# Reshaping and moving the piecewise loads of layer 1: pieces of 128 partitions by 1 KB, issued at one step of a block

## The chip, the cores and the metric

The kernel runs on one core of one Trainium2 chip. A core has five engines that work side by side, each through its own queue of instructions in order: TensorE (PE in the profile, with its weight loads as PEld), VectorE (DVE), ScalarE (ACT), GpSimd (POOL) and SyncE (SP), which here issues nearly all the transfers (DMA). The metric is the device time of one execution in microseconds; lower is better.

## What is computed

The input x has 8 images of 512 channels by 32 x 32 points (t = 1024 tokens), all float32. Two layers follow each other, each with a group normalization first and a residual sum at the end. Cut to what matters:

```python
# layer 0: xf = _gn(x)
qkv = einsum('oc,bct->bot', qkv_w, group_norm(xf)) + qkv_b      # 8 heads of 64 channels
a = softmax(q.T k / sqrt(64)) v
x = x + einsum('oc,bct->bot', proj_w, xf + a) + proj_b
# layer 1: xf = _gn(x)
attn = einsum('bhdq,bhdT->bhqT', q, k) * scale                  # q, k, v = w_q xf, w_k xf, w_v xf
attn = softmax(einsum('gh,bhqT->bgqT', w_head, attn))           # the heads are mixed before the softmax
attn = instance_norm(attn) * gamma + beta                       # over queries and keys of one head
out = einsum('bhqT,bhdT->bhqd', attn, v).reshape(b, t, c)
x = x + (out @ w_proj.T + b_proj)
```

The mixing of the heads is what makes layer 1 heavy in transfers: scores of all 8 heads have to stand on the partitions of one matmul, and they are brought there by DMA.

## The kernel before

Layer 0 (lines up to 1261) runs first over all images and leaves its result in DRAM, in the tensors x1_0 to x1_7. Layer 1 (from 1264) then takes the images b = 0 to 7 one after the other. The order of instructions on each engine is the order in which the program writes them (a manual schedule, line 576); a framework adds the waits that the tiles need.

**One image of layer 1.** The 1024 queries are cut into 8 blocks p of 128. The loop runs over p = 0 to 8, and in each over four steps t = 0 to 3 (`step`, line 1839). Block p makes the scores of its queries, and mixes, exponentiates, flips and sums up what block p - 1 made, so the work is spread over three blocks:

- `scores` (1624) makes one of eight parts of block p; two parts in each step. ScalarE copies them from PSUM to a tile raw, one for each half kh of the keys (line 1643; two raw tiles in all, so that a block's copies wait until the transfers out of the block before are done).
- `regroup` (1645, issue on line 1648) brings a slice s of raw into the tile re by two transfers of 256 KB, r = 0 and 1, 128 rows of 2 KB each. Step 1 regroups (kh, s) = (0,0) and (0,1), step 2 (0,2), step 3 (0,3) and then (1,0), (1,1), (1,2), (1,3): 16 transfers in a block, ten of them in step 3. There is one tile re, so slice s is overwritten only after the mix of the block before has read it.
- `mix` (1658) mixes the heads: slice t of block p - 1 in step t. Its matmuls (1665) read re, ScalarE takes the exponential (1675).
- `flip` (1680) and `moments` (1692) are VectorE's transposes (1687) and statistics (1698); `values` (1702) multiplies with v (1714); `leave` (1722) copies the result out. `totals` (1746) of block p - 2 comes in step 1 with a reciprocal on line 1761, and the transfer of its inverse sums, rzb, is issued by GpSimd (1771).

Block 8 has no scores of its own; it only ends block 7, and next to it run the first products of the next image's k projection (`k_go`; matmuls on line 1383).

**The pieces.** While image b runs, the inputs of image b + 1 are loaded in pieces of 128 KB. The list `self.pieces` holds them in order: 16 pieces of y (`y_piece`, 1334: x1 of the next image, 2 MB, into the tile y), then 14 pieces of the k weights (`left_piece`, 1299: 1.8 MB of combined weights, from DRAM into the tile left_k). Image 7 has no successor and loads 8 pieces of w_proj instead (`p_piece`, 1324). `piece(n)` (1652) issues the next n. It is called at the end of steps 1 and 2 of every block from 1 on:

```python
                if p >= 1 and t in (1, 2):
                    self.piece(2 if p < 5 or t == 2 else 3)
```

So blocks 1 to 4 issue the 16 y pieces, four in each, and blocks 5 to 7 the 14 k pieces, five, five and four. In image 7 blocks 1 and 2 issue the eight w_proj pieces, and no block after them issues any. y is normalized in block 5 (`normalize1`, at slots 20 to 23), and left_k is read from the last step of block 7 on.

A y piece covers 32 partitions with 4 KB each (a whole row of 1024 tokens); a k piece and a w_proj piece cover 64 partitions with 2 KB each.

**The queue.** Pieces and regroups are issued by SP in program order. In the compiled program each transfer of SP also waits until the eighth before it has landed, so at most eight are under way. A regroup that waits for scores holds up everything behind it on SP.

Of the kernel before, what the change touches and what calls it, by code (L numbers as in the profile page):

```python
# [18 lines left out]
P = 128  # L19
# [448 lines left out]
def tile_two_attention_layers(  # L468
# [20 lines left out]
    B, C, T = x_d.shape  # L489
    H = w_head.shape[0]  # L490
    D = C // H
# [11 lines left out]
    x1_d = [dram.tile([C, T], F32, tag=f"x1_{b}", name=f"x1_{b}") for b in range(B)]  # L503
# [190 lines left out]
    with ExitStack() as l0:  # L694
# [21 lines left out]
        for c in range(NCC):  # L716
# [5 lines left out]
        HC = C // 2  # L722
# [4 lines left out]
        left_d = {  # L727
            which: dram.tile([P, 7 * 2 * HC], F32, tag=f"left_{which}", name=f"left_{which}")
            for which in SOURCES
        }  # L730
        left_t = {}

        def left_tile(which, b):
            t = wpool.tile([P, 7, 2, HC], F32, tag="left", name=f"left_{which}_{b}")
            left_t[which] = t
            return t
# [527 lines left out]
    with ExitStack() as l1:  # L1264
# [21 lines left out]
        y_t, qo_t, k_t, v_t = ({0: t["1"]} for t in (n_t, q_t, k_t, v_t))  # L1286
        w_t = {}
# [3 lines left out]
        HC = C // 2  # L1291
# [7 lines left out]
        def left_piece(key, i):  # L1299

            if i == 0:
                left_tile(key)
            f, r = i // 2, i % 2 * D
            return nc.sync.dma_start(
                out=w_t[key][r : r + D, f],
                in_=left_d[key[0] + "1"][r : r + D, f * 2 * HC : (f + 1) * 2 * HC],
            )

        def load_left(key, t=None):
# [14 lines left out]
        def p_piece(i):  # L1324

            if i == 0:
                left_tile(("p", B - 1))
                w_t["p", B - 1] = w_t["p", B - 1][:, :NCC]
            c, r = i // 2, i % 2 * D
            return nc.sync.dma_start(  # L1330
                out=w_t["p", B - 1][r : r + D, c], in_=w_projT[c * P + r : c * P + r + D]
            )

        def y_piece(b, i):

            if i == 0:
                y_t[b] = shared.tile([P, NCC, T], F32, tag="n", name=f"y_{b}")
            c, r = i // 4, i % 4 * 32
            return nc.sync.dma_start(
                out=y_t[b][r : r + 32, c], in_=x1_d[b][c * P + r : c * P + r + 32, :]  # L1340
            )

        def normalize1(b, c):
# [101 lines left out]
        def k_leave():  # L1445
            for fn in due:
                fn()
            due.clear()
# [167 lines left out]
        class Attention1:  # L1616
# [222 lines left out]
            def step(self, p, t, ag):  # L1839

                if p >= 1 and t == 3:
                    self.mix(p - 1, 3)
                if p < NT:
                    self.scores(p, 2 * t)
                    self.scores(p, 2 * t + 1)
                if t == 1 and p >= 2:
                    self.totals(p - 2)
                if t == 1 and p >= 1:
                    self.flip(p - 1, 0)
                    self.moments(p - 1, 0)  # L1850
                if t == 0 and p >= 2:
                    self.values(p - 2, 0, 1)
                    self.leave(p - 2, 0)
                if p >= 1 and t < 3:
                    self.mix(p - 1, t)
                ag.run(4 * p + t - 0.5)
                if 1 <= t <= 2 and p >= 2:
                    self.values(p - 2, 1, t - 1)
                    if t == 2:
                        self.leave(p - 2, 1)  # L1860
                if t == 3 and p >= 1:
                    self.values(p - 1, 0, 0)
                if t == 0 and p >= 2:
                    self.sums(p - 2)
                    if p % 2 == 0 and p >= 4:
                        self.divide(p // 2 - 2)
                k_leave()
                if p >= 1 and t:
                    self.flip(p - 1, t)
                    self.moments(p - 1, t)  # L1870
                if p < NT:
                    for kh, s in (
                        (), ((0, 0), (0, 1)), ((0, 2),), ((0, 3), (1, 0), (1, 1), (1, 2), (1, 3)),
                    )[t]:
                        self.regroup(kh, s)
                if p >= 1 and t in (1, 2):
                    self.piece(2 if p < 5 or t == 2 else 3)
                ag.run(4 * p + t)

        def load_wv(b):  # L1880
# [7 lines left out]
        for b in range(B):  # L1888
# [10 lines left out]
            if more:  # L1899
                a.pieces += [lambda i=i: y_piece(b + 1, i) for i in range(4 * NCC)]  # L1900
                a.pieces += [lambda i=i: left_piece(("k", b + 1), i) for i in range(14)]
                for c in range(NCC):
                    ag.at(20 + c, lambda c=c: normalize1(b + 1, c))

                def k_go(*ms):
                    if not kp:
                        kp.append(k_projection(b + 1))
                    for m in ms:
                        kp[0].products(m)
                        due.append(lambda m=m: kp[0].leave(m))  # L1910

                kp = []
                ag.at(4 * NT - 0.5, lambda: right_tile(b + 1))
                ag.at(4 * NT - 0.5, lambda: k_go(1))
                ag.at(4 * NT, lambda: right_y(b + 1, [0, 1]))
                ag.at(4 * NT + 0.5, lambda: k_go(2))
                ag.at(4 * NT + 1, lambda: right_y(b + 1, [2, 3]))
                ag.at(4 * NT + 1, lambda: left_p(b))
                ag.at(4 * NT + 1.5, lambda: k_go(6))
                ag.at(4 * NT + 2.5, lambda: k_go(7))  # L1920
            else:
                a.pieces += [lambda i=i: p_piece(i) for i in range(2 * NCC)]
# [113 lines left out]
```

## Time and profile before

| what | value |
|---|---|
| median of 3 runs | 4119.6 us (4113.11 to 4122.85) |
| the profiled execution | 4120.51 us |
| its span, first to last instruction | 4118.7 us |
| mean granted TensorE clock | 0.992 |
| transfers `re<-raw` | 1024 of 256 KB |
| transfers `y<-x` in pieces | 112 of 128 KB |
| transfers `left_k<-left_k` in pieces | 98 of 128 KB |
| share of queue 1 (SP's) of 16 DMA engines' span | 43.7% |

How to read the profile: the page gives busy time per engine, and the span in 40 equal slices, each digit being tenths of busy time (9 is 90% or more). "Waits" list who waited for whom: engine, line of the waiter, what released it, total us, how often, the longest. "Windows" list the busy us of each engine in a stretch of time, with the clock granted to TensorE, the mean busy share of the 16 DMA engines, and GB/s moved. A timeline row gives start, length, engine, line, operation, tiles, and in brackets the idle time ahead and what ended it. Lines are those of the kernel. Busy times of matmuls are modelled, so a busy TensorE isn't TensorE at its peak.

### The profile page before, as it was taken

The page shows a single profiled execution, that of the slowest core. Times are in us where ns is not written, and L with a number is a line of the kernel's source. Part 1 is how long each engine was busy: PE and PEld are TensorE (multiplying, and loading weights), DVE is VectorE, ACT ScalarE, POOL GpSimd, SP SyncE. Part 2 cuts the span into 40 slices and gives each one's busy share as a digit, 9 for nine tenths or more (in the row PEclk, how much of TensorE's full clock was granted, in tenths as well). Part 3 has the DMA queues.
Part 4 walks back from the last instruction along what each step waited for, and adds up shares of the span by engine and source line. Part 5 has one row for each costly group of instructions (what it writes and reads, how often), then busy time and mean ns, then how long its engine had stood idle before and what let it go on. Part 6 is the DMA issues. An engine that isn't in the chain of part 4 may idle for free. (4 is left out here: it accounts for less than half of the span.)

```text
span 4118.7 us, 96170 instructions
## 1 busy us (share of the span) xinstructions
PE 3945.7 (96%) x41932; PEld 1822.9 (44%) x41932; DVE 2876.9 (70%) x4340; ACT 1961.1 (48%) x2431; POOL 71.2 (2%) x126
## 2 busy tenths in 40 slices
PE   8999999999999999999999999998998999999997
PEld 4353535353534343334434434444444444445344
DVE  4748484757575666648859768769678589498596
ACT  1717272636354544427437347256166165174273
POOL 0000000000000000000000000000000000000000
PEclk9999999999999999999999999999999999999998
DMA  3313131212121111139649558469288287397384
GB/s 128 106 51 109 49 114 44 88 47 88 47 85 49 56 62 65 70 106 216 175 115 220 147 146 209 137 162 218 97 190 212 88 209 183 113 215 191 108 207 119
DMA packets 251101, 519.12 MB, mean 126 GB/s; under 512 B 49840, under 2 KB 57008, under 8 KB 244016
## 3 DMA queue, kind: packets, MB, share of 16 engines
q1 hardware_dynamic: 244128, 497.96, 43.7%
q0 software_dynamic: 6544, 14.94, 1.7%
q8 instruction: 331, 5.42, 0.6%
q14 instruction: 98, 0.80, 0.1%
HBM read 197.16 MB, written 46.92 MB: 59 GB/s over the span
## 5 line engine op out<-in xcount | busy, mean ns | idle before, releaser
L1698 DVE BATCH_NORM_STATS2 bn<-e 128x6 f32<-128x512 f32 x1024 | 631.5, 671 | 0.0
L1643 ACT COPY raw<-s 128x1024 f32<-128x1024 f32 x480 | 465.7, 1022 | 322.0 <-PE s L1631 158.4
L1687 DVE STREAM_TRANSPOSE et<-e 128x2048 f32<-128x2048 f32 x256 | 585.6, 2288 | 34.5 <-ACT e L1675 34.5
L1086 ACT ACTIVATE e<-s 128x1024 f32<-128x1024 f32 x512 | 497.2, 1026 | 233.2 <-PE s L1081 232.8
L1675 ACT ACTIVATE e<-m 128x1024 f32<-128x1024 f32 x512 | 496.6, 1022 | 196.0 <-issue 58.8
L1714 PEld LDWEIGHTS a<-et,v 128*64 128x64 f32 x16384 | 499.7, 138 | 194.1 <-issue 193.3
L1631 PE MATMUL s<-k,q 64*64 64x512 f32 x4096 | 534.4, 616 | 43.2 <-ACT e L1675 37.5
L1714 PE MATMUL a<-et,v 128*64 128x64 f32 x16384 | 531.7, 224 | 4.9 <-DVE et L1687 4.9
L1094 DVE TENSOR_TENSOR zacc<-zacc,e 128x1024 f32<-128x1024 f32 x384 | 468.8, 1221 | 90.2 <-ACT e L1086 68.0
L1081 PE MATMUL s<-q,k 64*64 64x512 f32 x4096 | 490.1, 593 | 2.3 <-ACT e L1086 2.3
L1107 PE MATMUL a<-e,v 64*64 64x512 f32 x4096 | 484.1, 589 | 0.0
L1665 PE MATMUL m<-re,wmix 32*32 32x512 f32 x8192 | 368.6, 612 | 83.1 <-DMA re<-raw 34.0
L1631 PEld LDWEIGHTS s<-k,q 64*64 64x64 f32 x4096 | 124.1, 133 | 364.7 <-ACT e L1675 162.5
L1107 PEld LDWEIGHTS a<-e,v 64*64 64x64 f32 x4096 | 156.7, 133 | 282.8 <-issue 282.5
L1081 PEld LDWEIGHTS s<-q,k 64*64 64x64 f32 x4096 | 147.9, 133 | 275.2 <-issue 240.5
L1458 PE MATMUL pv<-wv,y 128*128 128x512 f32 x480 | 212.1, 597 | 0.0
L1665 PEld LDWEIGHTS m<-re,wmix 32*32 32x32 f32 x8192 | 80.8, 103 | 212.2 <-ACT raw L1643 92.1
L1730 ACT COPY q<-a 64x256 f32<-64x256 f32 x256 | 94.0, 367 | 146.9 <-PE a L1714 144.1
L1458 PEld LDWEIGHTS pv<-wv,y 128*128 128x128 f32 x480 | 89.3, 190 | 117.7 <-issue 109.5
L1761 DVE RECIPROCAL rz<-z 32x32 f32<-32x32 f32 x64 | 22.1, 346 | 160.7 <-PE z L1750 150.9
L1462 ACT COPY v<-pv 128x512 f32<-128x512 f32 x30 | 17.6, 586 | 218.5 <-PE pv L1458 218.5
L1092 DVE TENSOR_TENSOR zacc<-e,e 128x1024 f32<-128x1024 f32 x64 | 78.3, 1224 | 55.9 <-ACT e L1086 55.9
(314 smaller groups left out, 3948.7 us busy)
## 6 DMA issues: line engine op xcount, KB each, us to landing
re<-raw SPq DMA_DIRECT2D x1024, 256.0 KB
left_q<-left_q SPq DMA_DIRECT2D x17, 1792.0 KB
left_p<-left_p SPq DMA_DIRECT2D x17, 1792.0 KB
left_k<-left_k SPq DMA_DIRECT2D x10, 1792.0 KB
x<-in_x_dram SPq DMA_DIRECT2D x32, 512.0 KB
rzb<-zd SPq DMA_DIRECT2D x128, 128.0 KB
x<-x SPq DMA_DIRECT2D x64, 256.0 KB
left_v<-left_v SPq DMA_DIRECT2D x8, 1792.0 KB
```

The lines of the kernel that those rows point to most:

```text
L1081: nc.tensor.matmul(ps[c * D : c * D + D, m], k[r, hp, k0 : k0 + D], q[r, hp, ts(f, FB)], start=True, stop=True,)
L1086: nc.scalar.activation(e[i], ps, AF.Exp, scale=S0 * S0)
L1094: nc.vector.tensor_add(zacc[g], zacc[g], e[i])
L1107: nc.tensor.matmul(acc[g][a][m * D : m * D + D], v[rows, kc, ts(2 * hp + m, D)], e[i][rows, m], start=(kc == 0), stop=(kc == NG - 1),)
L1458: nc.tensor.matmul(ps[:, m], y_t[b][:, c, ts(2 * i + m, P)], w[:, c], start=(c == 0), stop=(c == NCC - 1),)
L1631: nc.tensor.matmul(ps[c * D : c * D + D, m], qo_t[b][r, p, hp, ts(c, D)], k_t[b][r, hp, ts(kh, FB)], start=True, stop=True,)
L1643: nc.scalar.copy(dst, ps)
L1665: nc.tensor.matmul(ps[a // 2][c * 32 : c * 32 + 32, a % 2].rearrange("p (r kb k) -> p r kb k", r=2, k=32), wmix[rows].rearrange("p g i -> ...
L1675: nc.scalar.activation(e[:, :, 2 * h : 2 * h + 2].rearrange("p r a k -> p a r k"), ps[h].rearrange("p a (r k) -> p a r k", r=2), AF.Exp,)
L1687: nc.vector.transpose(self.et[p, u].rearrange("p kb (r st a) g q -> p st kb r (a g q)", r=2, st=2)[:, st], self.e[p, s].rearrange("p r a ( ...
L1698: nc.vector.bn_stats(self.bn[p][:, s, a], e[:, :, a].rearrange("p r k -> p k r"))
L1714: nc.tensor.matmul(acc[two * D : two * D + D, s].rearrange("p (x q) -> p x q", q=4), v_t[b][:, kb, ts(g, D)], et[:, kb, :, g], start=(kb = ...
```

## The change

Two things change, both for the pieces of layer 1 alone.

Their shape: every piece now covers all 128 partitions with 1 KB each. A y piece is a quarter of the tokens of 128 channels, a k piece or a w_proj piece half of the columns of 128 rows. The number of pieces, their order, their bytes and the tiles they fill stay the same.

Their place: they are issued at the end of step 0, four in blocks 1 to 4, five (in the end four) in blocks 5 to 7, rather than at the ends of steps 1 and 2. Step 0 regroups nothing. On SP they therefore stand behind the last regroups of the block before, (1,0) to (1,3), and ahead of the first of the block's own, (0,0). The order of instructions on the other engines stays.

```diff
@@ left_piece
-            f, r = i // 2, i % 2 * D
+            f, h = i // 2, i % 2
             return nc.sync.dma_start(
-                out=w_t[key][r : r + D, f],
-                in_=left_d[key[0] + "1"][r : r + D, f * 2 * HC : (f + 1) * 2 * HC],
+                out=w_t[key][:, f, ts(h, HC)],
+                in_=left_d[key[0] + "1"][:, (2 * f + h) * HC : (2 * f + h + 1) * HC],
             )
@@ p_piece
-            c, r = i // 2, i % 2 * D
+            c, h = i // 2, i % 2
             return nc.sync.dma_start(
-                out=w_t["p", B - 1][r : r + D, c], in_=w_projT[c * P + r : c * P + r + D]
+                out=w_t["p", B - 1][:, c, ts(h, HC)], in_=w_projT[ts(c, P), ts(h, HC)]
             )
@@ y_piece
-            c, r = i // 4, i % 4 * 32
+            c, r = i // 4, i % 4
             return nc.sync.dma_start(
-                out=y_t[b][r : r + 32, c], in_=x1_d[b][c * P + r : c * P + r + 32, :]
+                out=y_t[b][:, c, ts(r, HC)], in_=x1_d[b][ts(c, P), ts(r, HC)]
             )
@@ step
-                if p >= 1 and t in (1, 2):
-                    self.piece(2 if p < 5 or t == 2 else 3)
+                if p >= 1 and t == 0:
+                    self.piece(4 if p < 5 else 5)
                 ag.run(4 * p + t)
```

Here P = 128, D = 64, HC = 256, and `ts(i, n)` is the slice from i n to (i + 1) n.

## The prediction

> **What bounds the kernel now.** I read the page first: engines, slices, costliest groups.
>
> ```profile
> PE 3945.7 (96%) x41932; PEld 1822.9 (44%) x41932; DVE 2876.9 (70%) x4340; ACT 1961.1 (48%) x2431; POOL 71.2 (2%) x126
> ...
> DMA  3313131212121111139649558469288287397384
> GB/s 128 106 51 109 49 114 44 88 47 88 47 85 49 56 62 65 70 106 216 175 115 220 147 146 209 137 162 218 97 190 212 88 209 183 113 215 191 108 207 119
> ```
>
> TensorE is busy 96% of the span, so only its gaps can be won. The DMA row rises to 8 and 9 tenths in the second half: that is layer 1, from about 1800 us on, the only part that the change touches. So I asked who waits for transfers there (the waits of ScalarE and TensorE from 1800 us on; columns: total us, times, longest).
>
> ```profile
> ACT raw L1643 <- DMA re<-raw: 116.0, 37, 4.3
> ...
> PE m L1665 <- DMA re<-raw: 34.0, 23, 3.8
> ```
>
> These are regroups (`re<-raw`), not pieces: the pieces can cost time only by delaying regroups. The control for that is in the trace itself. Image 7, the last, loads nothing for a successor; its pieces (w_proj) end in block 2, so its blocks 3 to 6 run without pieces. I cut the span at the reciprocal of L1761, which falls in step 1 of each block, and asked for busy time by window (columns: window, length, busy us of each engine with counts, granted clock, DMA share, GB/s). First two of image 7 without pieces, then two of image 3 with y pieces, then the sum line for the 14 such windows (blocks 3 and 4 of images 0 to 6), then the sum line for the seven windows of block 6 with k weight pieces.
>
> ```profile
> 3961.12:3983.41 22.29, 21.60 (x454) 11.11 (x454) 20.37 (x32) 16.68 (x21) 1.15 (x2) 1.00 0.81 202
> 3983.41:4005.76 22.35, 21.58 (x454) 11.05 (x453) 21.50 (x33) 16.73 (x21) 1.15 (x2) 1.00 0.83 203
> ...
> 2765.64:2789.77 24.13, 21.61 (x454) 11.11 (x455) 21.51 (x32) 16.61 (x21) 1.15 (x2) 1.00 0.92 215
> 2789.77:2813.35 23.58, 21.79 (x454) 11.29 (x454) 21.20 (x32) 16.67 (x21) 1.15 (x2) 1.00 0.90 215
> ...
> sum 329.81, PE 303.74 PEld 156.14 DVE 298.94 ACT 232.90 POOL 16.16; mean PE 21.70 PEld 11.15 DVE 21.35 ACT 16.64 POOL 1.15
> ...
> sum 162.71, PE 149.96 PEld 77.57 DVE 142.61 ACT 115.13 POOL 8.08; mean PE 21.42 PEld 11.08 DVE 20.37 ACT 16.45 POOL 1.15
> ```
>
> The engines do the same work in all of them; only length and DMA share differ. Image 7's four windows average 22.36 us; the 14 with four y pieces 329.81/14 = 23.56; the seven with five k pieces 162.71/7 = 23.24. So pieces cost 1.20 us in a y block and 0.88 in a k block. Length times DMA share, averaged over the rows: 18.33 us of DMA work without pieces, 21.41 with y pieces, 21.36 with k pieces. A y piece thus costs 3.08/4 = 0.77 us of all 16 engines, a k piece 3.03/5 = 0.61. About 4 us of a block are free of DMA work without pieces; with them the block is nearly bound by transfers.
>
> Block 7 into 8 is worse, because block 8 has no scores to cover a late regroup. TensorE's timeline of image 3, then of image 6, at that place (start, length, what, idle before):
>
> ```profile
> 2881.33 2.02 PE L1665 MATMUL m<-re,wmix 32*32 32x512 f32 x32 [4.05 <-issue]
> 2883.28 5.44 PE L1383 MATMUL pk<-y,left_k 128*128 128x512 f32 x8
> ...
> 3761.83 1.30 PE L1665 MATMUL m<-re,wmix 32*32 32x512 f32 x32 [2.35 <-DMA re<-raw]
> 3763.05 3.70 PE L1383 MATMUL pk<-y,left_k 128*128 128x512 f32 x8
> ```
>
> After a 4 us gap the same eight matmuls take 5.44 us instead of 3.70: the wait is paid again in clock. The seven intervals at this place average 26.09 us, the best is 24.06.
>
> **What the Trainium skill says.** "SBUF — State Buffer", section "Door 1: The DMA port swizzle": partitions 0 to 31 and 0 to 63 reach the same 8 of 16 ports, 0 to 127 reach all (189, 196 and 328 GB/s at 1 MiB). The trace agrees in the mean: 131 KB in 0.77 us is 170 GB/s for 32-partition pieces and 215 for 64. For the new shape there is a witness: the layer 0 weight blocks are 128 rows of 1 KB, 128 KB each. The window in which eight of them run almost alone:
>
> ```profile
> 73.60:77.00 3.40, 3.40 (x10) 1.49 (x9) 1.59 (x3) 1.17 (x2) 0.00 (x0) 1.00 0.93 303
> ```
>
> 303/0.93 = 326 GB/s of busy time, 0.40 us a piece. "DMA: Bandwidth & Descriptors", section "Issuing engines are not separate DMA queues": all transfers end on the same 16 engines and interleave; the summed shares above fit. Same page, "Why small descriptors are slow (HBM only)": about 3 cycles more per packet; my estimate from it is 4 x (1024/32 + 3) = 140 against 131 cycles, 7% for cutting 4 KB into 1 KB. No run here shows it alone. "TensorE: Matmul & The Clock Gate", section "Why this matters for your kernels": no idle gaps over about 3 us; the 5.44 against 3.70 us agrees.
>
> **The change part by part.** Nothing is added or removed: as many pieces of 128 KB, as many bytes; the orders of TensorE, VectorE, ScalarE and GpSimd are the same, only SP's differs.
>
> Shape. Priced alone, a piece falls to 0.40 us (row above). Beside regroups it stretches: image 7's blocks move about 200 GB/s at a share of 0.82, 244 GB/s of busy time, so 131/244 = 0.54 us. I take 0.5 and keep both ends. A y block then has 4 x 0.5 = 2.0 us of piece work for 3.08, a k block 2.5 for 3.03. What that is worth: read as a threshold, about 2 us of piece work are hidden now (3.08 - 1.20 = 1.88; 3.03 - 0.88 = 2.15) and the rest costs one for one, so a y block wins up to 1.20 and a k block about 0.4. Read in proportion (1.20/3.08 and 0.88/3.03), they win 0.42 and 0.15.
>
> Place. Now two pieces stand between the regroups of step 1 and that of step 2 and two (or three and two) before those of step 3, ahead of the regroups that the next block's first mix and first raw copy wait for. After the change all stand on SP between the eight regroups that end step 3 and the first regroup of step 1. The eight are ahead of them in the queue, so the urgent ones lose a competitor. Each transfer on SP waits for the eighth before it, so the four pieces issue as those eight land, when DMA would run dry until step 1's raw copies are done. What is moved past: the four regroups of step 1 and the two of step 2 (first used a block later) now stand behind the pieces, by at most 4 x 0.54 = 2.2 us, nothing if DMA is free. GpSimd's rzb load of step 1 meets the same backlog; its value is used blocks later. On SP 16 regroups of about 0.6 us and four or five issues of 0.4 to 0.6 fill some 12 us of 22: SP itself isn't the bound. No new wait comes to bear: the y tile's last reader (v_pair in block 0) is issued a block earlier, the k tile's an image earlier. y is complete two steps sooner for its normalization, the k weights two steps sooner for their product. Taking place and shape together I put a y block at 0.9 won and a k block at 0.4. For block 7 into 8, where a gap also costs clock, I take 1.2 of the 26.09 - 24.06 = 2.03 us; both ends 0.4 and 2.03.
>
> Sum. Per image 0 to 6: blocks 1 to 4 (y) 4 x 0.9 = 3.6; blocks 5 and 6 (k) 0.8; block 7 1.2: 5.6 us, times 7 = 39. Image 7: two blocks of four w_proj pieces, 64 partitions each; block 2 measured 23.01, 0.65 over 22.36; I take 0.5 each, 1. Together 40 us. The profiled execution is 4120.5 us (span 4118.7), within 1 us of the median 4119.6: 4120.5 - 40 = 4080. In proportion only: 4 x 0.42 + 2 x 0.15 + 0.4 = 2.4, times 7 = 17 us, 4103. Everything won: 4 x 1.20 + 2 x 0.88 + 2.03 = 8.6, times 7, plus 1.3 = 61 us, 4059.
>
> **Rivals.**
> 1. The pieces vanish: in their new place they fall wholly into the DMA gap. For it: image 7's 4 us of free DMA time a block against 2.0 to 2.5 of pieces. Against: the gap isn't all at that place. 4059, with 4052 to 4064 around it.
> 2. Nothing changes: the ten regroups of step 3 set the waits by themselves, and the pieces only fill time beside them. For it: the waits name regroups alone. Against: image 7's blocks, same regroups, are 1.20 us shorter. 4120, within 8.
> 3. Slower: a transfer beside the regroups pays per row, not per byte. Place: the 16 engines in blocks 1 to 7. Regroup rows of 2 KB take about 17.2 us (18.33 less some 1.1 for rzb) over 128 rows per engine, 0.134 us each; if a 1 KB row costs as much, a piece of 8 rows per engine costs 1.07 us. With hidden room used up, that is 4 x 0.30 = 1.2 us more in a y block, 5 x 0.46 = 2.3 in a k block, 1.8 in block 7: 11.2 an image, 79 in all, 4199. It decides from 0.70 us a piece on (the mean of 16 at 0.77 and 14 at 0.61), 0.087 us a row. For it: no 1 KB row in this trace runs beside regroups. Against: alone, such rows take 0.40/8 = 0.05 us.
> That the change doesn't do what it says is excluded by the order of instructions: the pieces stand there, in that shape.
>
> **How the numbers follow.** Forecast (4064 to 4103, middle 4080) 0.62; all won, 4059: 0.12; nothing, 4120: 0.11; slower, 0.15, spread from 4128 to 4199. What a measurement of this kernel can tell from no change is about 0.2%, 8 us. So faster 0.74, same 0.11, slower 0.15. The range takes the forecast, most of the first rival and the lower half of the second, some 0.79: 4054 to 4120.
>
> **What would show it.** In the profile after: windows of blocks 3 and 4 near 22.7 us instead of 23.56, DMA share times length near 20.3 instead of 21.41; block 6 near 22.8; the waits ACT raw and PE m on re<-raw well under 116 and 34 us; the gaps before the first mix of block 8 all near 2.3 us and its eight matmuls at 3.7. A DMA product of 21.4 or more in y blocks would say that the shape saved nothing; a product that falls while the length stays, that regroups bind by themselves; a growing gap in block 8, that the place is wrong.

## The result and the profile after

| | before | after |
|---|---|---|
| median of 4 runs each on the same chip | 4121.23 us | 4077.56 us |
| lowest to highest | 4113.11 to 4130.34 | 4076.32 to 4082.87 |
| profiled execution | 4120.51 us | 4077.14 us |

The ratio is 0.9899, with a 95% interval of [0.9886, 0.9913]: the changed kernel is faster by about 1%. The forecast was 4080.

The page of the kernel after, engines and DMA row:

```profile
PE 3936.3 (97%) x41932; PEld 1821.1 (45%) x41932; DVE 2876.3 (71%) x4340; ACT 1961.7 (48%) x2431; POOL 71.0 (2%) x126
...
DMA  3313131212111111238639548468379287387384
```

No engine has fewer instructions, and their busy times are within 0.3% of those before. What is gone is idle time. Next, the waits from 1800 us on (engine, line, what it waited for: us in total, times, longest):

```profile
PE m L1665 <- DMA re<-raw: 45.8, 41, 3.9
ACT raw L1643 <- DMA re<-raw: 5.8, 4, 2.9
```

ScalarE's copies no longer wait for regroups: 116.0 us in 37 waits became 5.8 in 4. The mix matmuls wait on regroups for 45.8 us rather than 34.0. This is no new loss: the page's idle time ahead of line 1665 from all causes fell from 83.1 to 51.2 us. More of what is left is put down to a regroup, because the copies ahead of it are now on time. So the 45.8 can't be set beside the 34.0; the 51.2 beside the 83.1 can.

The windows between reciprocals of line 1761: blocks 3 and 4 of image 3, then the sum over all 14 such windows of images 0 to 6, then the sum over the seven of block 6 (columns as in the prediction):

```profile
2746.55:2768.77 22.22, 21.60 (x454) 11.11 (x454) 21.51 (x32) 16.71 (x21) 1.15 (x2) 1.00 0.90 229
2768.77:2792.75 23.98, 21.60 (x454) 11.11 (x455) 21.15 (x32) 16.68 (x21) 1.15 (x2) 1.00 0.95 227
...
sum 318.11, PE 302.13 PEld 155.73 DVE 298.85 ACT 233.76 POOL 16.10; mean PE 21.58 PEld 11.12 DVE 21.35 ACT 16.70 POOL 1.15
...
sum 157.75, PE 150.97 PEld 77.70 DVE 142.54 ACT 116.48 POOL 8.06; mean PE 21.57 PEld 11.10 DVE 20.36 ACT 16.64 POOL 1.15
```

318.11/14 = 22.72 us a y block (23.56 before) and 157.75/7 = 22.54 in block 6 (23.24). Eight of the 14 now have the 22.2 to 22.5 us of a block without pieces; two, one of them the second row, still take 23.8 and 24.0 (e8 shows why). Length times DMA share is 20.43 us in the y blocks, 21.41 before. The place where block 8 begins, TensorE's timeline of image 4 (start, length, what, idle before):

```profile
3145.47 2.02 PE L1665 MATMUL m<-re,wmix 32*32 32x512 f32 x32 [3.92 <-DMA re<-raw]
3147.42 5.27 PE L1383 MATMUL pk<-y,left_k 128*128 128x512 f32 x8
```

and of image 6:

```profile
3720.76 1.15 PE L1665 MATMUL m<-re,wmix 32*32 32x512 f32 x32 [2.03 <-DMA re<-raw]
3721.84 3.70 PE L1383 MATMUL pk<-y,left_k 128*128 128x512 f32 x8
```

The first eight matmuls of the k projection (line 1383) take 3.70 us at the full granted clock; in image 4 they take 5.27, at a mean granted clock of 0.70. As before the change, some images wait almost 4 us here and then lose clock, and some don't. The mean of block 7 to block 8 over seven images is 26.15 us; it was 26.09. This part of the forecast did not come.

Where the time went, from window means over images 0 to 6 (the row for blocks 0 and 1 is the period of an image, 293.32 before and 288.01 after, less the others; in the changed kernel a block's pieces are issued within some 3 us of the reciprocal, before and after it, so a row can hold pieces of two blocks):

| part | before | after | won, us | forecast |
|---|---|---|---|---|
| blocks 0 and 1 | 119.08 | 118.61 | 0.47 | 0.9 |
| block 2 | 23.60 | 22.56 | 1.04 | 0.9 |
| blocks 3 and 4, each | 23.56 | 22.72 | 0.84 | 0.9 |
| block 5 (y is normalized in it) | 24.44 | 23.02 | 1.42 | 0.4 |
| block 6 | 23.24 | 22.54 | 0.70 | 0.4 |
| block 7 to block 8 | 26.09 | 26.15 | -0.06 | 1.2 |
| from block 8 on | 29.75 | 29.69 | 0.06 | 0 |
| an image | 293.32 | 288.01 | 5.31 | 5.6 |

5.31 x 7 = 37.2 us, and 1.7 in image 7: 38.9. The profile after is 43.4 us shorter. The other 4.4 us stand ahead of the first reciprocal of layer 1 (1862.49 before, 1858.06 after); over the twelve profiles of the study that moment lies anywhere from 1858.1 to 1863.1, so I don't count them to the change.

### The profile page after: what moved, and what is told of

Read it like the earlier page. It is cut to its first block, busy times and chain, and to the rows that moved or that the text cites. A ratio compares the mean times of both kernels' runs of the same rounds, so it can differ in the third digit from the quotient of the medians.

```text
span 4075.4 us, 96121 instructions
## 1 busy us (share of the span) xinstructions
PE 3936.3 (97%) x41932; PEld 1821.1 (45%) x41932; DVE 2876.3 (71%) x4340; ACT 1961.7 (48%) x2431; POOL 71.0 (2%) x126
## 3 DMA queue, kind: packets, MB, share of 16 engines
q8 instruction: 331, 5.42, 0.6%
## 4 chain that ended last, share of the span: by engine, by line
PE 76%; DVE 12%; DMA 5%; ACT 4%; issue 2%; SPq 1%; ACTq 0%; DVEq 0%
PE s L1081 11%; PE a L1107 11%; PE pk_p L899 5%; DVE et L1687 5%; PE pq_p L899 5%; DVE bn L1698 5%; PE pv L1458 5%; DMA re<-raw 5%; PE a L1714 5%; PE pv_p L899 5%; PE pp_p L899 5%; PE pk L1383 5%; PE s L1631 4%; PE pq L1383 4%; PE pp L1383 4%; PE m L1665 4%
## 5 line engine op out<-in xcount | busy, mean ns | idle before, releaser
L1665 PE MATMUL m<-re,wmix 32*32 32x512 f32 x8192 | 365.5, 607 | 51.2 <-DMA re<-raw 45.8
L899 PE MATMUL pv_p<-left_v,tmp 128*128 128x256 f32 x512 | 113.1, 379 | 0.0
```

Of the source, the lines that this page charges most:

```text
L899: nc.tensor.matmul(out, st, mv, start=start, stop=(k == 1), skip_group_check=True)
L1665: nc.tensor.matmul(ps[a // 2][c * 32 : c * 32 + 32, a % 2].rearrange("p (r kb k) -> p r kb k", r=2, k=32), wmix[rows].rearrange("p g i -> ...
```

## Experiments

Two questions were open. Which half of the change does it, shape or place? And what sets the wait at block 8, which the change left as it was? Kernels e1 to e4 ran on one chip (before there: 4116.77 us), after_again and e5 to e7 on another (4114.42), e8 and e9 on a third (4113.64). All times are medians, and each ratio is to the runs of before on the same chip. The changed kernel itself was not run beside e1 to e4; its ratio is 0.9899 and 0.9907 on two other chips. A profile is one execution: those of e2 and e5 are the fastest of their six (7 and 6 us under the median), that of e3 the slowest (5 us over it).

### e1: the shape alone

The new pieces in their old place.

```diff
-                if p >= 1 and t == 0:
-                    self.piece(4 if p < 5 else 5)
+                if p >= 1 and t in (1, 2):
+                    self.piece(2 if p < 5 or t == 2 else 3)
```

> The new shape at the old place (ends of steps 1 and 2). Before 4121, after 4078. Theory work (the gain is the smaller DMA work of a piece, wherever it stands): most of the 43 us, about 4088, and DMA share times length in y blocks near 20.4 as in the changed kernel. Theory place (the gain is that no piece stands between the regroups of steps 1 to 3): little, 4112 or more, with the DMA product also near 20.4 but the blocks near 23.4.

4088.37 us, ratio 0.9937 [0.9924, 0.995]. Blocks 3 and 4 take 22.87 us at a DMA product of 20.93, block 6 takes 23.08. The shape alone wins 0.69 of a y block's 1.20 us and only 0.16 of block 6's 0.88. ScalarE's waits on regroups fall from 116.0 to 70.3 us. The time is the 4088 that the first theory named, but e2 and e3 contradict its "wherever it stands", and the product fell less than it said.

### e2: the place alone

The old pieces, of 32 and 64 partitions, in the new place.

```diff
@@ y_piece
-            c, r = i // 4, i % 4
+            c, r = i // 4, i % 4 * 32
-                out=y_t[b][:, c, ts(r, HC)], in_=x1_d[b][ts(c, P), ts(r, HC)]
+                out=y_t[b][r : r + 32, c], in_=x1_d[b][c * P + r : c * P + r + 32, :]
...
```

> The old shape (32 and 64 partitions) at the new place (end of step 0). Theory work: DMA product in y blocks stays near 21.4 and little is won, 4108 or more. Theory place: the pieces fall into the time in which DMA would run dry, so nearly all is won, 4085 or less. If both parts count alike, about 4100.

4082.98 us, ratio 0.9922 [0.9909, 0.9934]. The waits from 1800 us on, and the sum over the 14 windows of blocks 3 and 4:

```profile
PE m L1665 <- DMA re<-raw: 43.1, 42, 3.8
ACT raw L1643 <- DMA re<-raw: 10.3, 6, 2.8
```

```profile
sum 318.32, PE 303.07 PEld 155.60 DVE 298.76 ACT 233.62 POOL 16.10; mean PE 21.65 PEld 11.11 DVE 21.34 ACT 16.69 POOL 1.15
```

318.32/14 = 22.74 us, the 22.72 of the whole change, while the DMA product stays high: 21.04 here, 21.52 in block 6 (22.55 us). This is as the theory of place had it. So pieces that keep the DMA engines nearly as busy as before cost little once nothing urgent stands behind them; whether they cost nothing, these runs can't tell, since the intervals of e2's ratio and the change's overlap by little. Shape (0.63%) and place (0.78%) sum to 1.4%, more than the change's 1.0%: in part they take away the same waits.

### e3: new shape, wrong place

The same new pieces, issued in step 3 ahead of the ten regroups instead of behind them.

```diff
+                if p >= 1 and t == 3:
+                    self.piece(4 if p < 5 else 5)
...
-                if p >= 1 and t == 0:
-                    self.piece(4 if p < 5 else 5)
```

> The new shape, all pieces of a block at its step 3 ahead of the ten regroups there, the worst place by my account: 4 x 0.5 = 2 us of transfers in front of the regroups that the next first mix and first raw copy wait for. Theory place: 0.7 to 1.2 us a block over 49 blocks, 4112 to 4136, and waits of ACT raw on re<-raw come back. Theory work: the queue works off the same transfers in any order, 4078 to 4086.

4098.44 us, ratio 0.9955 [0.9941, 0.9968]. Its waits from 1800 us on, and the same 14 windows:

```profile
ACT raw L1643 <- DMA re<-raw: 84.1, 32, 4.9
PE m L1665 <- DMA re<-raw: 37.0, 29, 3.7
```

```profile
sum 320.49, PE 302.09 PEld 155.67 DVE 298.80 ACT 232.60 POOL 16.09; mean PE 21.58 PEld 11.12 DVE 21.34 ACT 16.61 POOL 1.15
```

The kernel loses half of the gain. That lies between the two forecasts: over the 4086 of the theory of work, under the 4112 of the theory of place. Blocks 3 and 4 take 22.89 us, block 6 takes 23.27 (22.54 after), block 7 to block 8 takes 26.71. ScalarE's waits are back. Yet the DMA product is the least of all, 19.63. The product alone is not what sets the length of a block; what stands ahead of an urgent regroup counts.

### e4: 32 partitions with rows of 1 KB

As after, but a y piece covers 32 partitions with four rows of 1 KB each: as many bytes and rows, a quarter of the partitions.

```diff
-            c, r = i // 4, i % 4
+            r, h = i // 4, i % 4
-                out=y_t[b][:, c, ts(r, HC)], in_=x1_d[b][ts(c, P), ts(r, HC)]
+                out=y_t[b][ts(r, 32), :, ts(h, HC)],
+                in_=x1_d[b].rearrange("(c p) t -> p c t", p=P)[ts(r, 32), :, ts(h, HC)],
```

> As the changed kernel, but a y piece covers 32 partitions with four rows of 1 KB each (four channel groups) rather than 128 partitions with one; bytes, row size, number of rows and place stay, k pieces as changed. If the partitions covered set a piece's price: DMA product in y blocks back near 21.4, and where work counts some 0.6 us a block in 28 blocks, 4094; if rows or bytes set it: as the changed kernel, 4078, product 20.4.

4080.03 us, ratio 0.9914 [0.9899, 0.9929]. Blocks 3 and 4 of image 0:

```profile
1886.02:1908.40 22.38, 21.61 (x454) 11.11 (x455) 21.59 (x32) 16.72 (x21) 1.15 (x2) 1.00 0.95 219
1908.40:1931.03 22.63, 21.61 (x454) 11.12 (x454) 21.18 (x33) 16.67 (x21) 1.15 (x2) 1.00 0.97 225
```

The DMA share is 0.95 and 0.97, and the blocks are short all the same. Over the 14 windows the product is 22.11, so a piece costs (22.11 - 18.33)/4 = 0.95 us of all engines against 0.53 after: with bytes and rows the same, fewer partitions make a piece dearer, as the prediction had it. (These windows hold on average 2.9 such pieces and 1.4 k pieces, so one with 32 partitions is dearer still.) Its forecast of 4094 for that case is wrong: the dearer piece costs almost no time here, 22.84 against 22.72 us a block.

### after_again and e5: are the k pieces of block 7 behind the wait at block 8?

after_again is the changed kernel once more, for comparison on this chip: 4076.5 us, ratio 0.9907 [0.9891, 0.9923].

> The changed kernel itself, beside the other three on the same chip, as their measure. Both theories: ratio to before near the first 0.990, that is some 41 us less than before.

In e5 blocks 5 and 6 issue seven k pieces each and block 7 none.

```diff
-                    self.piece(4 if p < 5 else 5)
+                    self.piece(4 if p < 5 else 7)
```

> As the changed kernel, but the 14 k pieces stand seven and seven in blocks 5 and 6, none in block 7. If k pieces in block 7 make the gap before the first mix of block 8: the interval from block 7 to 8 falls from 26.1 to about 24.1, less what blocks 5 and 6 lose, some 10 us less than the changed kernel. If the gap is set by the regroup itself and by whatever else lands on one DMA engine then: the interval stays at 25.5 to 26.5, time within 5 us of the changed kernel.

4081.72 us, ratio 0.992 [0.9905, 0.9935]. Without pieces in block 7 its DMA product falls from 21.80 (after_again) to 19.94, but block 7 to block 8 only from 25.99 to 25.40 us, and three of seven images still take 26.1 to 27.1. The 0.6 us are within what this interval scatters: e4, whose k pieces are those of the change, has 25.25. The interval is just below the 25.5 to 26.5 of the second theory. The k pieces are not what makes the long waits.

### e6: rows of 2 KB

y pieces of 256 KB, 128 partitions with 2 KB each, two in a block instead of four.

```diff
-            c, r = i // 4, i % 4
+            c, r = i // 2, i % 2
-                out=y_t[b][:, c, ts(r, HC)], in_=x1_d[b][ts(c, P), ts(r, HC)]
+                out=y_t[b][:, c, ts(r, FB)], in_=x1_d[b][ts(c, P), ts(r, FB)]
...
-                    self.piece(4 if p < 5 else 5)
+                    self.piece(2 if p < 5 else 5)
...
```

> As the changed kernel, but y pieces of 256 KB, 128 partitions with 2 KB each, two in a block for four. If the row size matters beside the regroups: DMA product in y blocks down by some 0.3 to 0.5 us, time 4070 to 4078. If only bytes and partitions count: as the changed kernel, within 4 us.

4075.44 us, ratio 0.9908 [0.9892, 0.9924], against 4076.5 for rows of 1 KB. The product of blocks 3 and 4 is 20.13 (after_again 20.66), their length 22.81 (22.67). Five profiles with the 1 KB rows have products from 20.2 to 20.7, so doubling the row makes no difference that can be told at 128 partitions. Over 32 partitions it may: e4 with 1 KB has 22.11, e2 with 4 KB has 21.04, though their k pieces differ too.

### e7: the first k products ahead of block 8's first mix

The slots that hold the first eight matmuls of the next image's k projection run ahead of the mix that waits, in block 8 alone. This change of order is the only one against the kernel after.

```diff
+                if p == NT and t == 0:
+                    ag.run(4 * p + t - 0.5)
                 if p >= 1 and t < 3:
                     self.mix(p - 1, t)
```

> As the changed kernel, but in block 8 the first products of the next k projection (3.7 us of TensorE, which need no regroup) stand ahead of the first mix. If the gap there is a wait for the regroup (1,0) with nothing to do: the interval from block 7 to 8 falls from 26.1 to about 22.7, seven images, 20 to 28 us less than the changed kernel, and no cold clock in these windows. If the wait only moves behind the products: no change.

4059.88 us, ratio 0.9868 [0.9849, 0.9887]: the best of all, 17 us under after_again and 55 under before. TensorE's timeline at block 8 of image 4:

```profile
3127.79 3.95 PE L1714 MATMUL a<-et,v 128*64 128x64 f32 x128
3131.67 3.70 PE L1383 MATMUL pk<-y,left_k 128*128 128x512 f32 x8
3135.74 1.15 PE L1665 MATMUL m<-re,wmix 32*32 32x512 f32 x32 [0.38 <-DMA re<-raw]
```

The 3.70 us of k products now lie in the wait, which is down to 0.38 us, and they run at full clock. Block 7 to block 8 takes 24.03 to 24.05 us in every image. This wins (25.99 - 24.04) x 7 = 13.7 us, and (29.77 - 29.23) x 7 = 3.8 behind it, of which 17 arrive; 20 to 28 were expected, from an interval of 22.7. It can't come to that, as the window row of image 4 shows (columns as in the prediction, VectorE the third):

```profile
3115.36:3139.40 24.04, 22.31 (x446) 11.81 (x459) 23.76 (x34) 14.67 (x19) 1.15 (x2) 1.00 0.95 225
```

VectorE is busy for 23.76 of the 24.04 us. So a wait of TensorE that is short enough costs nothing: of 70 such intervals in the ten profiles without this edit, 16 had the k products in 3.70 us. Eleven of these followed waits of 2.03 to 2.62 us and took 24.04 to 24.07 us; the other five, after waits up to 3.05 us, took 24.24 to 24.49. What e7 wins is the longer waits and the clock lost behind a wait.

### e8: moving the instruction fetches

The intervals of block 7 to block 8 in after_again are 27.81, 24.38, 25.17, 25.31, 28.04, 26.07 and 25.14 us in images 0 to 6, and the profile after has the same two or three long ones. Something repeats with the program. In the DMA view of the kernel after, cut to the 8 us around that wait in image 4 (queue, kind: packets, MB, share of 16 engines), stands a packet that no line of the kernel issues:

```profile
q1 hardware_dynamic: 916, 1.67, 84.4%
q8 instruction: 1, 0.02, 0.7%
```

It is a fetch of instructions, 16 KB in one packet. In the packet records it starts at 3142.19 us and takes 0.88; others before it start at 3124.84, 3131.45 and 3136.90. To find out whether it matters, e8 repeats the sums over V of the first four heads in image 0, 32 tiny matmuls more. These shift where all later fetches fall, and change nothing in the blocks.

```diff
-            for g in range(H):
+            for g in [*range(H // 2), *range(H)]:
```

> The kernel after the change, but the sums over V of the first four heads are done twice in image 0 alone (32 extra matmuls of 128 instruction records, half of a 16 KB instruction fetch), which shifts by about half a period where in each block the fetches fall. Nothing else is changed. Theory A (the long wait before block 8's first mix comes of an instruction fetch that lands while the last regroup of block 7 is under way): the pattern over the images turns round. Block 7 to block 8 was 27.81, 24.38, 25.17, 25.31, 28.04, 26.07, 25.14 us in images 0 to 6; images 0 and 4 should fall to 25.5 or less, and at least one of images 1, 2, 3, 6 should rise to 26.5 to 28. Total 4072 to 4085. Theory B (the pieces and regroups themselves set the wait, or the weights of the block): the pattern stays, images 0 and 4 near 28 and the others within 0.5 us of these values. Total 4076 to 4080.

4080.09 us, ratio 0.9914 [0.9895, 0.9933]. The pattern turned:

| image | 0 | 1 | 2 | 3 | 4 | 5 | 6 |
|---|---|---|---|---|---|---|---|
| after_again: interval, us | 27.81 | 24.38 | 25.17 | 25.31 | 28.04 | 26.07 | 25.14 |
| fetch starts, us after block 7's reciprocal | 16.9 | 15.0 | 14.1 | 13.5 | 17.0 | 15.3 | 14.3 |
| e8: interval, us | 25.20 | 24.06 | 26.93 | 25.56 | 25.14 | 25.38 | 28.07 |
| fetch starts | 14.0 | 14.0 | 17.0 | 15.0 | 14.2 | 14.0 | 17.9 |

TensorE's timeline of e8 at block 8 of image 4, which waited 3.9 us in both runs of the kernel after, and of image 6:

```profile
3141.36 2.02 PE L1665 MATMUL m<-re,wmix 32*32 32x512 f32 x32 [2.19 <-DMA re<-raw]
3143.31 4.32 PE L1383 MATMUL pk<-y,left_k 128*128 128x512 f32 x8
```

```profile
3718.87 2.02 PE L1665 MATMUL m<-re,wmix 32*32 32x512 f32 x32 [3.77 <-DMA re<-raw]
3720.82 5.70 PE L1383 MATMUL pk<-y,left_k 128*128 128x512 f32 x8
```

The long waits left images 0 and 4 and went to images 2 and 6, with the fetch. How it delays a regroup shows in the landing signals of the second transfer of regroup (1,0), for which the mix waits, in the kernel after:

```
image 4, issued 3139.86: 3143.16 3143.30 3143.38 3143.42 ... 3143.55 3143.59 3143.64 | 3145.33
image 6, issued 3717.04: 3720.26 3720.34 3720.36 3720.36 ... 3720.61 3720.61 | 3720.62
```

A transfer has sixteen such signals. "DMA: Bandwidth & Descriptors" of the Trainium skill says in "Why a DMA increments its semaphore by 16 and not by 1" that the engines finish independently and that each signals behind its own data; these records agree. In image 4 fifteen are there within 0.49 us and the last comes 1.69 us later; in image 6 all sixteen come within 0.36. So by this reading one DMA engine is late, and the mix waits for it. The records don't say which engine a packet is on, so that the fetch sits on the late one is inferred.

The same measure over the ten profiles (all but the two with k first), 70 intervals: in the 19 cases where the last signal came over 1.4 us behind the fifteenth, the interval is 26.64 to 28.12 us, 27.45 in the mean. The other 51 have a mean of 25.24, and four of them are above 26.6, three of these in e3, where pieces stand ahead of this regroup. In each of the 19 a fetch starts 16.9 to 17.9 us after the reciprocal; among the 51 there are three such, all at 17.9, and they did no harm.

The same marks the blocks of 24 us. The changed kernel has 32 windows of blocks 3 to 6, image 7's among them. In five of them a fetch starts 15.5 to 18.3 us after the reciprocal (bounds chosen after looking at these profiles), and these take 23.81 to 24.16 us; no other takes over 23.28. In e8 the count is six, at 23.76 to 24.56, and no other is over 23.08. In image 7, where no pieces run, the long block is block 6 with 23.81 us in the changed kernel; in e8 it is block 5 with 23.83, and block 6 takes 22.36. TensorE waits there for a regroup too; first the changed kernel in block 6, then e8 in block 5:

```profile
3983.99 1.15 PE L1665 MATMUL m<-re,wmix 32*32 32x512 f32 x32 [1.63 <-DMA re<-raw]
3961.85 1.15 PE L1665 MATMUL m<-re,wmix 32*32 32x512 f32 x32 [1.64 <-DMA re<-raw]
```

### e9: the reorder on the kernel before

The edit of e7, made to the kernel before.

> The kernel before the change, with its old pieces in their old places, but with the k projections of block 8 ahead of the first mix, as in the earlier run with k first. Theory A (the gap before block 8's first mix has nothing to do with the pieces): block 7 to block 8 falls from 26.1 to about 24.0 us, so 2.1 x 7 + the lighter last image = 15 to 20 us less than before, ratio 0.9952 to 0.9964. Theory B (the reorder pays only with the changed pieces, because with the old ones the piece's own regroup wait comes later): within 5 us of before, ratio 0.9988 to 1.0012.

4100.05 us, ratio 0.9958 [0.9943, 0.9972]. Block 7 to block 8 takes 24.04 to 24.06 us in every image, from 26.09. So the loss at block 8 was there before the change, and covering the wait pays without the change too; the ratio is within the 0.9952 to 0.9964 of the first theory. The two gains multiply: 0.9907 x 0.9958 = 0.9866, and both together measured 0.9868.

## Why the prediction was right, and where not

**The total.** The sum was 40 us. The medians differ by 43.7 us in the first measurement and by 4114.42 - 4076.5 = 37.9 beside after_again; the windows of the profile show 38.9 that belong to the change. That the sum comes so near is partly luck: block 7 into 8 was to give 8.4 us and gave nothing, and blocks 5 and 6 gave (1.42 + 0.70 - 0.8) x 7 = 9.2 us more than forecast.

**The control.** Taking image 7's blocks without pieces as the floor was right in the main: with 1.20 us to win in a y block, 0.84 came in blocks 3 and 4 (forecast 0.9), and half of the 14 windows stand at 22.2 to 22.4 us, the 22.36 of the floor. But the four windows of that floor held no fetch at 15.5 to 18.3 us; in the changed kernel one of them does, and their mean is 22.77. Counting only windows without such a fetch, a y block took 23.30 us before (nine windows), 0.94 over image 7's, and 22.52 after (twelve), 0.10 over the 22.42 of image 7's three. So of the 1.20 us some 0.94 were the pieces' own cost, and nearly all of that is gone; most of what is left is the fetches.

**The price of a piece.** Forecast 0.5 us beside regroups; measured (20.43 - 18.33)/4 = 0.53. The rival that a 1 KB row costs as much as a 2 KB row in the regroups (1.07 us a piece) falls with it. e4 shows that the partitions set part of the price; e6 shows no effect of the row at 128 partitions. But the price isn't the piece's own: worked out in the same way, the same pieces cost (20.93 - 18.33)/4 = 0.65 us in their old place (e1) and (19.63 - 18.33)/4 = 0.33 ahead of the ten regroups (e3).

**Shape against place.** The working read the length of a block as a threshold on DMA work: some 2 us of pieces hidden, the rest paid one for one. This doesn't hold. e2 and e4 have DMA products of 21.0 to 22.1 us in blocks of 22.7 to 22.8; e3 has 19.6 in blocks of 22.9. What counts most is whether a piece is queued ahead of a regroup that someone needs soon. In the old place it was, and then a lighter piece helped (e1); in the new one its weight hardly counts. The forecast took place and shape together at 0.9 and so didn't suffer, but on the threshold alone e2 would have won much less than it did.

**The k blocks** were the term set too low: "I put ... a k block at 0.4" was derived from the small fall of DMA work. Block 6 won 0.70 us, and 0.69 with the place alone, 0.16 with the shape alone. Block 5 won 1.42: the forecast gave it block 6's cost of 0.88 without cutting its window, which stood at 24.44 before, 2.09 above the same window of image 7 (22.35).

**Block 7 into block 8** is the step that failed: "For block 7 into 8, where a gap also costs clock, I take 1.2 of the 26.09 - 24.06 = 2.03 us". Nothing was won there, and the sign named for it, gaps all near 2.3 us, didn't come. The step put these 2.03 us down to the pieces, without a control: its 24.06 was the best of seven intervals that all had pieces. e5 takes the pieces of block 7 away and wins 0.6, within the scatter; e8 moves the long waits from image to image by shifting instruction fetches; e9 wins the 2 us on the kernel before with its pieces as they were. What the runs show in its place: the 2 us are the cost of waits that grow past some 2.6 us (19 of the 23 over 3.2 us have a fetch at 16.9 to 17.9 us) and of the lower clock behind most waits. Why the clock falls after some waits of 2 us and not after others stays open.

**The waits named as signs.** ScalarE's fell as forecast, from 116.0 to 5.8 us. TensorE's on regroups rose from 34.0 to 45.8 against the forecast; 20.6 of these are the seven waits ahead of block 8's first mix, and with the k products ahead (e7) the total is 23.1, the longest 2.2. The sign was badly chosen, since waits that were put down to other causes before are now put down to regroups: from all causes TensorE waited 83.1 us ahead of line 1665 before and 51.2 after.

## What to carry to other kernels

Where prefetches share a queue with transfers that the next step waits for, first ask what stands behind each prefetch: behind the urgent ones a heavy piece cost next to nothing here, ahead of them a light one lost half of the gain. A floor taken from iterations that lack the suspected work is a good measure of what can be won in those iterations, but a wait at another place needs its own control. Where an engine must wait for a transfer, put independent work of its own queue into the wait: one call moved ahead won 14 to 17 us, with either kind of piece. And where single iterations of a loop are long without a cause in their own work, shift the program by a few instructions and see whether the long ones move.

## What the runs showed of the hardware

- Instruction fetches get in the way of data. The page counts 331 packets on q8 among the packets of the 16 DMA engines in the kernel after, 16 KB each (5.42 MB), 0.6% of the engines' span. Yet where one falls beside an urgent regroup, the last of that transfer's sixteen signals comes 1.4 to 1.9 us behind the fifteenth, and the wait for it is 3.7 to 4.2 us; in the shortest third of the 70 intervals it is 2.0 to 2.3. That fetches decide which images and blocks are long is shown by e8; how a packet of 0.9 to 1.2 us delays the transfer by more than its own length stays open.
- The clock suffers from shorter gaps than expected. "TensorE: Matmul & The Clock Gate" of the Trainium skill, section "Why this matters for your kernels", asks for no gaps over about 3 us. In the ten profiles, of 47 gaps of 2.03 to 3.15 us ahead of block 8's first mix only 16 were followed by eight k matmuls in 3.70 us; behind the other 31 they took 4.2 to 5.8. After all 23 gaps of 3.29 to 4.21 us they took 4.3 to 5.7. In e7 and e9, with at most 0.44 us of waiting left there, all 14 took 3.70. So about 2 us of idling can cost clock here, not always.
- A piece of 128 KB takes 0.53 us of all 16 DMA engines over 128 partitions and 0.95 or more over 32, both with 1 KB rows and issued at the same place. At other places the former takes 0.33 and 0.65: what a transfer adds to the busy time of the DMA engines depends on what runs beside it.
